# Moving VectorE's own sums, and the matmuls of other work, to other slots of a tanh-attention loop; attending in four key tiles at a time

## The chip, the cores and the metric

The kernel runs on one core of one Trainium2 chip. The metric is the device time of one execution in microseconds; three runs of the kernel before gave a median of 6138.88 us (6137.63 to 6139.3).

## What is computed

The input x is 8 images of 128 channels on a 36 x 36 grid. Layer 0 is a convolutional attention block with a residual. Layer 1 takes each image as 1296 tokens of 128 features and adds an attention whose score is a sum of tanh over the features, and then an expert-choice feed-forward layer. The part that takes most of the time is layer 1's attention:

```python
q = jnp.einsum('bld,ed->ble', x, Wq) + bq
k = jnp.einsum('bld,ed->ble', x, Wk) + bk
t = jnp.tanh(q[:, :, None, :] + k[:, None, :, :])
scores = jnp.einsum('bijd,d->bij', t, w) + bw[0]
attn = jax.nn.softmax(scores, axis=-1)
return jnp.einsum('bij,bjd->bid', attn, x)
```

For every image there are 1296 x 1296 pairs of tokens, and for each pair 128 values of tanh. Everything is float32.

## The kernel before

**The scores.** The kernel doesn't evaluate tanh pair by pair. It splits the features into small groups, of 5 and of 6 features, and writes the sum over a group as one fraction: a denominator and a numerator that are each a matrix product of a query factor (qf, two parts) with a key factor (kf). A group of 5 has 32 rows to contract over, a group of 6 has 64. The scores of a pair are the sum of all numerators divided by their denominators. The work is cut into *units*: one image b, one chunk c of 432 queries (three an image), one tile j of 128 keys (ten an image, and a remainder of 16 keys). A full unit has 12 *slots* k (`SLOTS`, L49 to L54); each slot does two groups at once on different rows of TensorE's array. They come in threes: k % 3 = 0 and 1 are groups of 5 (L53), k % 3 = 2 is groups of 6 (L54). A remainder unit has only two slots. The whole loop has 2928 slots (L1113).

**One slot.** The order of the instructions is written out by hand (L102). In slot p, `take_turns` (L1072) first lets other work copy out a result; then `numerators(p)` (L977) issues the matmuls n for this slot; `denominators(p + LAG)` (L960) issues the matmuls d three slots ahead, and on ScalarE the logarithm of d and, every second slot, the exponential of its negative, which is the reciprocal lq; `terms(p, ns)` (L982) multiplies n by lq on VectorE; and `matmul_turn` (L1077) lets other work issue matmuls.

**The sums.** `terms` has two ways. In the slots of `DVE_PAIRS` (L59), the groups of 6, VectorE multiplies the two numerators in place in PSUM and adds both into a running sum accd (L996 to L999). The first of these in a unit starts accd and has one addition less (L990 to L994). In the other eight slots VectorE multiplies out of PSUM into a buffer rp (three of them, L147), and GpSimd adds rp to a second running sum, accp (L1006 to L1012): the first rp is kept (k = 0), the second makes accp (k = 1). After a unit, `sums` (L1016) adds the halves of accp and accd on GpSimd, and ScalarE takes the exponential seven slots later (L1146, L1026). For a remainder unit, matmuls do the sum (`rem_scores`, L1039), issued in the following unit; they read rp.

**PSUM.** n and all the other work share four PSUM buffers (ps_n, L151): an n takes two, every other step takes one (`aux`, L159). The denominators have two buffers of their own (L149).

**The other work.** Behind the scores run generators in four lanes (L1067): query blocks and remainder sums (first_of_all), attending (urgent), gating (gates), and the next image's layer 0, tokens and keys (background). Each step issues a few matmuls into one aux buffer, yields `TAKE`, copies the result out one slot later at the earliest, and yields `matmuls()`. `take_turns` lets no lane but first_of_all copy in a slot of DVE_PAIRS. `matmul_turn` lets none but first_of_all issue matmuls in the slot before such a slot, nor while the balance is negative: every slot adds 400 (`PACE`), every matmul takes off its columns plus 20 (L282).

**Attending.** When all key tiles of a chunk have their exponentials, `attend` (L747) makes the weighted sum of the tokens, in four tiles of 108 queries. A tile needs 11 matmuls (10 key tiles and the remainder), issued by `weigh` (L737) in two parts, of 6 and of 5: the first part is copied to sums, the second added to it. For four tiles of the last chunk, early parts are done by `attend_early`.

Of the kernel before, what the change touches and what calls it, by code (L numbers as in the profile page):

```python
# [27 lines left out]
NKT = len(KT)  # L28
# [26 lines left out]
NP = len(SLOTS)  # L55
IN_TURN = [m + i for m in range(NF // 2) for i in (0, NF // 2)]
LAG = 3
SHIFT = 6.5
DVE_PAIRS = (2, 5, 8, 11)  # L59
PACE = 400  # L60


# [8 lines left out]
def kernel(  # L71
# [28 lines left out]
    nc = tc.nc  # L100
# [29 lines left out]
    with ExitStack() as loop, ExitStack() as score:  # L130
# [22 lines left out]
        def big_tile(name):  # L153
            return big.tile([128, NT * 128], F32, tag="big", name=name)
# [4 lines left out]
        def aux(name):  # L159
            return ps_n.tile([128, 512], F32, tag="n", name=name)  # L160
# [116 lines left out]
        def matmuls(rest=0):  # L277
            return (True, rest)
# [458 lines left out]
        def weigh(pa, i, some, es, xh, xr):  # L737

            for j in some:
                if j < NKT - 1:  # L740
                    e, v = es[j][:, i * T : (i + 1) * T], xh[:, j, :]
                else:
                    rows = slice(32 * i, 32 * i + REM)
                    e, v = es[j][rows, :T], xr[rows]
                bmm(pa, e, v, start=(j == some[0]), stop=(j == some[-1]))

        def attend(b, c, es):  # L747


            xh, _, xr = prepared[b]  # L750
            if c == 0:
                t2 = big_tile("t2").rearrange("p (t c) -> p t c", c=128)
                mv = two.tile([T, NT, 2], F32, tag="t2_mv", name="t2_mv")
                attended[b] = (t2, mv)
            t2, mv = attended[b]
            own = range(c * TPC, (c + 1) * TPC)
            for at in own:
                nc.sync.dma_start(t2[:T, at, :], tokd[b][at * T : (at + 1) * T])
            for i, at in enumerate(own):
                if i in early:  # L760
                    parts, sums = (order[NKT - 2 :],), early[i]
                else:
                    parts = (range(6), range(6, NKT))
                    sums = two.tile([T, C + 1], F32, tag="sums", name="sums")
                for some in parts:
                    pa = aux("pa1")[:T, : C + 1]
                    weigh(pa, i, some, es, xh, xr)
                    yield TAKE
                    if some[0] == 0:
                        nc.vector.tensor_copy(sums, pa)  # L770
                        yield matmuls()
                nc.vector.tensor_add(pa, pa, sums)
                inv = small.tile([T, 1], F32, tag="inv", name="inv")
                nc.vector.reciprocal(inv, pa[:, C : C + 1])
                nc.vector.scalar_tensor_tensor(
                    t2[:T, at, :], pa[:, :C], inv, t2[:T, at, :], ALU.mult, ALU.add
                )
                st = small.tile([T, 6], F32, tag="t2_st", name="t2_st")
                nc.vector.bn_stats(st, t2[:T, at, :])
                nc.vector.bn_aggr(mv[:, at, :], st)  # L780
                yield matmuls()
            if c == NCH - 1:
                prepared.pop(b)
            if b == NB - 1:
                yield from gate_logits(b, [c])

        def gating(b):
            yield from gate_logits(b, range(NCH))
            yield from gate_tokens(b)
# [114 lines left out]
        def residuals(n):  # L904

            for b in range(n):
                res.append(big_tile("res")[:, :N])
                nc.sync.dma_start(res[b], t2d[b])
                yield step()
# [11 lines left out]
        slots = []  # L921
# [4 lines left out]
        def prefetch(u):  # L926
            if u < len(units) and u not in kf_of:
                b, c, j = units[u]
                assert (b, j) in made
                n = 128 if j < NKT - 1 else 32  # L930
                kf = kfp.tile([128, NF, 128], F32, tag="kf", name="kf")
                nc.sync.dma_start(
                    kf[:, :, :n], kd[b][j].rearrange("p (q t) -> p q t", t=128)[:, :, :n]
                )
                kf_of[u] = kf
# [46 lines left out]
        def terms(p, ns):  # L982

            u, k = slots[p]
            lq = lq_of[u, k // 2]
            o = 2 * (k % 2)
            mult = nc.vector.tensor_mul
            rem = units[u][2] == NKT - 1
            if k in DVE_PAIRS and not rem:
                if k == DVE_PAIRS[0]:  # L990
                    live["d"] = acc.tile([128, CH], F32, tag="accd", name="accd")
                    mult(live["d"], ns[0], lq[:, o, :])
                    mult(ns[1], ns[1], lq[:, o + 1, :])
                    nc.vector.tensor_add(live["d"], ns[1], live["d"])  # L994
                else:
                    for h in range(2):  # L996
                        mult(ns[h], ns[h], lq[:, o + h, :])  # L997
                    for h in range(2):
                        nc.vector.tensor_add(live["d"], ns[h], live["d"])  # L999
            else:  # L1000
                rp = rpp.tile([128, 2, CH], F32, tag="rp", name="rp")
                for h, n in enumerate(ns):
                    mult(rp[:, h, :], n, lq[:, o + h, :])  # L1003
                if rem:
                    live.setdefault("rem", []).extend(rp[:, h, :] for h in range(len(ns)))
                elif k == 0:  # L1006
                    live["r"] = rp
                elif k == 1:
                    live["p"] = acc.tile([128, 2, CH], F32, tag="accp", name="accp")
                    nc.gpsimd.tensor_add(live["p"], live["r"], rp)  # L1010
                else:
                    nc.gpsimd.tensor_add(live["p"], live["p"], rp)  # L1012
            if k % 2 == 1:
                lq_of.pop((u, k // 2))
# [53 lines left out]
        balance = [0]  # L1068
# [3 lines left out]
        def take_turns(p, k):  # L1072
            for lane in lanes:
                if lane.due(p, False) and (k not in DVE_PAIRS or lane is first_of_all):
                    lane.run(p)

        def matmul_turn(p, k):  # L1077


            before = behind[0]  # L1080
            for lane in lanes:
                while lane.due(p, True) and behind[0] == before:
                    paced = balance[0] < 0 or k + 1 in DVE_PAIRS
                    if lane is not first_of_all and paced or lane is gates and urgent:
                        break
                    lane.run(p)
            balance[0] = min(balance[0] - (behind[0] - before) + PACE, 2 * PACE)
# [25 lines left out]
        for p, (u, k) in enumerate(slots):  # L1113
            b, c, j = units[u]
            rem = j == NKT - 1
            if k == 0:
                prefetch(u + 2)
                if c == 0 and j == 1:
                    if b > 0:
                        gates.append(gating(b - 1))  # L1120
                    if b == NB - 1:
                        gates.append(residuals(4))
                    if b + 1 < NB:
                        background.extend(
                            (normal(b + 1), conv_keys(b + 1), layer0(b + 1), tokens(b + 1),
                             keys(b + 1, range(NKT)))
                        )
            take_turns(p, k)
            ns = numerators(p)
            denominators(p + LAG)  # L1130
            terms(p, ns)
            if pending and pending[0][0] <= p:
                exps(p, *pending.popleft()[1:])
            last = p + 1 == len(slots) or slots[p + 1][0] != u

            if j == order[-1] and u + 1 < len(units) and k % 3:
                used = IN_TURN.index(SLOTS[k][0]) + 1
                if used < NF:
                    first_of_all.append(new_block(*units[u + 1][:2], IN_TURN[used]))
            elif j == order[-2] and last and u + 2 < len(units):  # L1140
                first_of_all.append(new_block(*units[u + 2][:2], IN_TURN[0]))
            matmul_turn(p, k)
            if last and rem:
                first_of_all.append(rem_scores(p, u, live.pop("rem")))
            elif last:
                pending.append((p + 7, u, sums(u)))  # L1146
        while pending:
            exps(p, *pending.popleft()[1:])
        take_turns(len(slots), 0)
        assert not first_of_all and not gates and not background  # L1150
        score.close()

# [205 lines left out]
```

The softmax here doesn't subtract the row's maximum and nothing guards it: scores larger than these inputs give would overflow.

## Time and profile before

| | |
|---|---|
| median of three runs | 6138.88 us |
| the profiled execution | 6140.74 us |
| its span, first to last instruction | 6139.0 us |
| before the first slot's numerators | about 162 us |
| the loop of 2928 slots | about 5824 us |
| the feed-forward layer after it | about 153 us |
| granted TensorE clock | 0.985 |
| numerators n, TensorE, 11520 matmul records | 3325.3 us busy |
| denominators d, TensorE, 11520 matmul records | 2991.6 us busy |
| products rp, VectorE, 3912 | 2173.3 us busy, 600 ns each |
| products n in place, VectorE, 1440 | 814.9 us busy, 608 ns each |
| additions to accd, VectorE, 1440 | 866.3 us busy, 602 ns each |
| additions to accp, GpSimd, 1440 | 2915.8 us busy, 2025 ns each |
| logarithms, ScalarE, 2928 | 2524.2 us busy, 878 ns each |
| exponentials of reciprocals, ScalarE, 1464 | 2398.2 us busy, 1638 ns each |

How to read the views: PE is TensorE's matmuls, PEld its weight loads, DVE is VectorE, ACT ScalarE, POOL GpSimd. A float32 matmul stands in the trace as two records, two passes over the same columns. In a line of time, the first number is the start in us from the span's start, the second the time from the first start to the last end of the instructions merged in it, and "x4" their number; at the end, in brackets, is how long the engine was idle and what ended that. In the list of waits, a line names the waiting engine, tile and line, then what it waited for, the time in all, how often, and the longest.

### The profile page before, as it was taken

What the parts mean: (1) busy time and instruction counts of PE and PEld (TensorE: products, weight loads), DVE (VectorE), ACT (ScalarE), POOL (GpSimd) and SP (SyncE); (2) the same over time, 40 slices, a digit from 0 to 9 for tenths busy, and PEclk for the clock granted to TensorE, in tenths of its full rate; (3) what the DMA queues carried; (4) which work ended last, traced back from release to release, by engine and by line L of the source; (5) the groups of instructions that cost most, each with busy time, mean ns of one, the idle gap of its engine ahead of it and who ended that gap; (6) DMA issues with size and microseconds to landing.
All of it is one profiled execution on the core that took longest, in us unless ns stands there. A gap on an engine that the chain in (4) does not pass through costs nothing.

```text
span 6139.0 us, 93072 instructions
## 1 busy us (share of the span) xinstructions
PE 5957.9 (97%) x33480; PEld 2862.1 (47%) x33480; DVE 4796.4 (78%) x9521; ACT 5279.9 (86%) x5371; POOL 4597.7 (75%) x2819
## 2 busy tenths in 40 slices
PE   7999999999999999999999999999999999999996
PEld 5454444544544445444455444454444544544443
DVE  4787878877788787877888777887778877788882
ACT  1888898888988888889998889888898888999990
POOL 4777777777787777778778786877777777787870
PEclk9999999999999999999999999999999999999997
DMA  1210011100110002100111001110011100110008
GB/s 44 70 37 22 25 62 38 34 25 28 68 43 20 26 27 71 39 24 23 44 55 39 22 24 59 44 39 22 20 65 40 34 25 28 58 50 29 28 20 297
DMA packets 151519, 270.87 MB, mean 44 GB/s; under 512 B 45648, under 2 KB 76752, under 8 KB 151056
## 3 DMA queue, kind: packets, MB, share of 16 engines
q1 hardware_dynamic: 151056, 264.92, 13.0%
q8 instruction: 264, 4.33, 0.3%
q14 instruction: 199, 1.63, 0.1%
HBM read 200.41 MB, written 64.19 MB: 43 GB/s over the span
## 4 chain that ended last, share of the span: by engine, by line
PE 77%; ACT 7%; DVE 6%; issue 6%; POOL 2%; DMA 1%; SPq 0%; DVEq 0%; POOLq 0%; ACTq 0%
PE n L949 37%; PE d L949 12%; PE pa L284 7%; PE pc L284 5%; ACT lq L972 5%; PE s L284 3%; PE pk L284 3%; PE pq L284 3%; DVE rp L1003 2%; DVE n L997 1%; DVE accd L999 1%; PE d L954 1%; ACT lq L975 1%; DMA w<-in_weight_dram 1%; PE n L954 1%
## 5 line engine op out<-in xcount | busy, mean ns | idle before, releaser
L1012 POOL TENSOR_TENSOR accp<-accp,rp 128x864 f32<-128x864 f32 x1440 | 2915.8, 2025 | 1041.0 <-DVE rp L1003 948.8
L949 PE MATMUL n<-qf,kf 32*128 32x432 f32 (+1 forms) x11520 | 3325.3, 574 | 46.5 <-ACT e L1032 13.3
L949 PE MATMUL d<-qf,kf 32*128 32x432 f32 (+1 forms) x11520 | 2991.6, 561 | 38.7 <-ACT lq L972 38.2
L972 ACT ACTIVATE lq<-d 128x864 f32<-128x864 f32 x2928 | 2524.2, 878 | 542.6 <-PE d L949 512.1
L1003 DVE TENSOR_TENSOR rp<-n,lq 128x432 f32<-128x432 f32 x3912 | 2173.3, 600 | 743.5 <-PE d L949 542.8
L975 ACT ACTIVATE lq<-lq 128x1728 f32<-128x1728 f32 (+1 forms) x1464 | 2398.2, 1638 | 46.3
L949 PEld LDWEIGHTS n<-qf,kf 32*128 32x128 f32 (+1 forms) x11520 | 1206.4, 184 | 1600.3 <-DVE rp L1003 581.5
L949 PEld LDWEIGHTS d<-qf,kf 32*128 32x128 f32 (+1 forms) x11520 | 1090.0, 185 | 422.1 <-issue 224.7
L997 DVE TENSOR_TENSOR n<-n,lq 128x432 f32<-128x432 f32 x1440 | 814.9, 608 | 142.1 <-PE n L949 88.5
L999 DVE TENSOR_TENSOR accd<-n,accd 128x432 f32<-128x432 f32 x1440 | 866.3, 602 | 24.6
L1010 POOL TENSOR_TENSOR accp<-rp 128x864 f32<-128x864 f32 x240 | 485.2, 2022 | 197.7 <-DVE rp L1003 195.6
L711 POOL TENSOR_SCALAR qf<-qf,cs_s 128x432 f32<-128x432 f32 x192 | 260.9, 1365 | 45.0 <-ACT qf L710 44.4
L284 PEld LDWEIGHTS pa<-xh,e 128*108 128x108 f32 x1920 | 222.5, 174 | 131.1 <-DVE rp L1003 56.0
L1021 POOL TENSOR_TENSOR accd<-accp,accd 128x432 f32<-128x432 f32 x240 | 265.2, 1105 | 18.8
L1019 POOL TENSOR_TENSOR accp<-accp 128x432 f32<-128x432 f32 x240 | 264.4, 1102 | 16.7
L284 PE MATMUL pa<-xh,e 128*108 128x129 f32 x1920 | 262.9, 283 | 8.7 <-ACT e L1032 5.2
L284 PE MATMUL s<-q,k 128*116 128x432 f32 x480 | 230.3, 568 | 1.7 <-DVE q L316 1.4
L284 PEld LDWEIGHTS pk<-xT,a_k 128*128 128x128 f32 x1408 | 171.2, 192 | 107.0 <-DVE n L997 33.7
L462 POOL TENSOR_TENSOR tot<-tot,e 116x432 f32<-116x432 f32 x192 | 212.0, 1104 | 6.0 <-ACT e L471 4.6
L471 ACT ACTIVATE e<-s 116x432 f32<-116x432 f32 x240 | 124.9, 520 | 98.3 <-PE s L284 97.9
L284 PE MATMUL pa<-e,vw 116*128 116x432 f32 x480 | 204.6, 549 | 0.0
L284 PE MATMUL pk<-xT,a_k 128*128 128x128 f32 (+1 forms) x1408 | 202.5, 287 | 0.1
(213 smaller groups left out, 3788.4 us busy)
## 6 DMA issues: line engine op xcount, KB each, us to landing
kf<-kd SPq DMA_DIRECT2D x239, 512.0 KB
kd<-ks SPq DMA_DIRECT2D x158, 256.0 KB
w<-in_weight_dram SPq DMA_DIRECT2D x32, 1024.0 KB
wk_t<-wk_t_d SPq DMA_DIRECT2D x7, 768.0 KB
wv_t<-wv_t_d SPq DMA_DIRECT2D x7, 768.0 KB
wq_t<-wq_t_d SPq DMA_DIRECT2D x7, 768.0 KB
x<-in_x_dram SPq DMA_DIRECT2D x8, 648.0 KB
t<-tokd SPq DMA_DIRECT2D x96, 54.0 KB
```

Of the source, the lines that this page charges most:

```text
L284: mm(out, lhsT, rhs, **kw)
L711: nc.gpsimd.tensor_scalar(qf[:, 1, :], qf[:, 0, :], cs_s[:, q : q + 1], None, ALU.mult)
L949: mm(outs[h][:, :CH], kf[rows[h], q, :], qf_of[b, c, q][rows[h], part, :], start=True, stop=True)
L972: nc.scalar.activation(lq[:, o : o + n, :], d[:, :n, :CH], AF.Ln)
L975: nc.scalar.activation(some, some, AF.Exp, scale=-1.0)
L997: mult(ns[h], ns[h], lq[:, o + h, :])
L999: nc.vector.tensor_add(live["d"], ns[h], live["d"])
L1003: mult(rp[:, h, :], n, lq[:, o + h, :])
L1010: nc.gpsimd.tensor_add(live["p"], live["r"], rp)
L1012: nc.gpsimd.tensor_add(live["p"], live["p"], rp)
L1019: nc.gpsimd.tensor_add(s[:, 0, :], s[:, 0, :], s[:, 1, :])
L1021: nc.gpsimd.tensor_add(d, s[:, 0, :], d)
```

## The change

The slots of VectorE's own sums become the first of each three, k = 0, 3, 6, 9, groups of 5. GpSimd's sums then begin at k = 1 and k = 2. Since other work may issue no matmuls in the slot ahead of these, its matmuls now come in k % 3 = 0 and 1 and no longer in the groups of 6; the comparison wraps at the unit's end. The two slots of a remainder unit count as places 1 and 11 for the lanes. Attending is done in three parts, of 4, 4 and 3 key tiles, with the middle one added to sums by one more instruction on VectorE; the four tiles with early parts keep theirs.

```diff
-DVE_PAIRS = (2, 5, 8, 11)
+DVE_PAIRS = (0, 3, 6, 9)
...
-                    parts = (range(6), range(6, NKT))
+                    parts = (range(4), range(4, 8), range(8, NKT))
...
-                    if some[0] == 0:
-                        nc.vector.tensor_copy(sums, pa)
+                    if some is not parts[-1]:
+                        if some is parts[0]:
+                            nc.vector.tensor_copy(sums, pa)
+                        else:
+                            nc.vector.tensor_add(sums, pa, sums)
                         yield matmuls()
...
-                elif k == 0:
+                elif k == 1:
                     live["r"] = rp
-                elif k == 1:
+                elif k == 2:
                     live["p"] = acc.tile([128, 2, CH], F32, tag="accp", name="accp")
...
-                    paced = balance[0] < 0 or k + 1 in DVE_PAIRS
+                    paced = balance[0] < 0 or (k + 1) % NP in DVE_PAIRS
...
-            take_turns(p, k)
+            place = (1, NP - 1)[k] if rem else k
+            take_turns(p, place)
...
-            matmul_turn(p, k)
+            matmul_turn(p, place)
...
-        take_turns(len(slots), 0)
+        take_turns(len(slots), 1)
```

## The prediction

> **Names.** A slot is one pair of numerator matmuls n(p), the denominators d(p+3) issued right after it on TensorE, and VectorE's products for p. Three slots make a *three*: 5a and 5b (groups of 5, 32-row matmuls) and 6 (group of 6, 64-row). A *behind step* is the background, attending or query-block work that TensorE does between two slots; its result is copied out in the next slot. The *pair slot* is the one of each three in which VectorE multiplies in place in PSUM and then adds both halves into accd (DVE_PAIRS); in the other two it multiplies into rp and GpSimd adds.
>
> **What bounds the kernel now.** First the page: its shares of busy time and its chain.
>
> ```profile
> PE 5957.9 (97%) x33480; PEld 2862.1 (47%) x33480; DVE 4796.4 (78%) x9521; ACT 5279.9 (86%) x5371; POOL 4597.7 (75%) x2819
> ...
> PE 77%; ACT 7%; DVE 6%; issue 6%; POOL 2%; DMA 1%; SPq 0%; DVEq 0%; POOLq 0%; ACTq 0%
> ```
>
> TensorE carries the chain, but its 97% includes matmuls that started and then stood. So next I read the waits, for what TensorE stands on before n.
>
> ```profile
> POOL accp L1012 <- DVE rp L1003: 948.8, 648, 6.9
> PEld n L949 <- DVE rp L1003: 581.5, 1032, 1.5
> ...
> PEld n L949 <- DVE accd L999: 198.5, 472, 1.6
> ...
> DVE rp L1003 <- PE rem L1045: 22.2, 24, 1.1
> ```
>
> Numerators wait for VectorE to free their PSUM buffers: there are four, an n takes two, a behind step takes one. GpSimd mostly waits for work. Last, one three in order of time, with a behind step (pc) in slot 6 and one in 5a. TensorE:
>
> ```profile
> 1066.35 0.99 PE L949 MATMUL n<-qf,kf 64*128 64x432 f32 x4
> ...
> 1068.01 1.27 PE L284 MATMUL pc<-xwin,wk_t 128*128 128x198 f32 x6
> 1069.21 0.65 PE L949 MATMUL n<-qf,kf 32*128 32x432 f32 x2
> ...
> 1070.26 1.27 PE L284 MATMUL pc<-xwin,wk_t 128*128 128x198 f32 x6
> 1071.46 0.63 PE L949 MATMUL n<-qf,kf 32*128 32x432 f32 x2
> ...
> 1072.40 1.00 PE L949 MATMUL n<-qf,kf 64*128 64x432 f32 x4
> ```
>
> and VectorE in the same stretch:
>
> ```profile
> 1067.55 1.12 DVE L997 TENSOR_TENSOR n<-n,lq 128x432 f32<-128x432 f32 x2
> 1068.58 1.24 DVE L999 TENSOR_TENSOR accd<-n,accd 128x432 f32<-128x432 f32 x2
> 1069.73 0.34 DVE L312 COPY k<-pc 128x187 f32<-128x187 f32 x1
> 1070.30 1.12 DVE L1003 TENSOR_TENSOR rp<-n,lq 128x432 f32<-128x432 f32 x2 [0.23 <-PE n L949]
> ```
>
> Differences of starts give TensorE's prices: slot 6 takes 1.66 us (1066.35 to 1068.01), a pc step 1.20, a 5 slot 0.94 (1071.46 to 1072.40). VectorE's: the pair slot starts at 1067.55; the first half is free when the first add ends, 1068.58 + 0.60 = 1069.18, 1.63 us after the pair's start; the whole pair takes 2.27. That is the point of this profile: n of 5a starts at 1069.21, when **two things end together**, the behind step and the first add. Slot 6 plus its behind step (2.86 us) covers the pair's hold on PSUM almost exactly. Over the whole trace, of 518 5a slots after such a pair, 260 have the second n starting 55 ns after the first add's end; so that wait is real and comes last half the time.
>
> I sorted 959 threes by which slots have behind steps and averaged the time between the n's. None: 138, 4.75 us. Only 6: 106, 5.49. Only 5a: 66, 4.82. Both: 508, 6.34. All three: 87, 6.84. Others: 54, about 6.3. Prologue (162 us) and tail (153 us) don't change.
>
> **What the Trainium skill says.** "Trainium Kernel Development and Optimization", Performance Expectations: matmul busy time is a poor measure, because matmuls are pipelined. The trace agrees: 97% busy, with 581.5 us of waits on rp inside. "TensorEngine Tiling (Array Packing)", Key Properties: a change of tiling mode drains TensorE. It agrees: inside a mode passes start 0.36 us apart, but a 5 slot's second passes start at 1071.93 and slot 6 only at 1072.40. "TensorE: Matmul & The Clock Gate", Part 3: matmuls start in program order, only weight loads move ahead. So a second n that waits holds up both d's and the behind step after it. The trace shows it: at 1069.21 the d's start after the n's.
>
> **The change, part by part.** (1) *The pair slot moves from 6 to 5a; behind steps move from (6, 5a) to (5a, 5b).* The amounts of work and the number of mode changes in a three stay the same; what covers the pair's hold changes. Start 5a at 0. Its n's end at 0.99, and the pair starts at 1.09 (as 1069.21 to 1070.30). First add ends: 1.09 + 1.63 = 2.72; the second n of 5b starts 0.055 later, 2.78. TensorE has been done with 5a (0.94) and its behind step (1.20) at 2.14: it stands **0.64 us**. The buffers leave no way round: two are held by the pair, one by the behind step (its copy is queued behind the pair on VectorE, as the 0.34 us COPY at 1069.73 is now), one by 5b's first n. Then 5b 0.94, its behind step 1.20, slot 6 1.66: 2.78 + 3.80 = 6.58 us, against 6.05 in the three shown. Slot 6's own n's don't wait: their buffers come free at about 4.6, before 4.92. One pair in four is the first of its unit (L990 to 994): it writes straight into accd and frees its first half after one multiplication, so there only TensorE's work counts, 2.14 + 3.80 = 5.94. Mean: (3 x 6.58 + 5.94)/4 = 6.42.
>
> The 6.34 measured for "both" holds longer steps and stray waits, 0.29 above 6.05. Some of these go: n of slot 6 waits on rp now, with no behind step ahead of it (its stretch to the next behind step averages 1.96 us against 1.65 at best); afterwards it has one. I keep 0.09 of the 0.29, bounds 0 and 0.29. So 6.51: +0.17 x 508 = **+86 us** (bounds +41 and +188).
>
> The other threes by the same steps. *None*: slot 6's second n now needs the pair's second half, at 1.09 + 2.27 + 0.06 = 3.42, and runs 1.64 from there: 5.06; first pairs about 4.6; mean 4.95, +0.20 x 138 = +28. *Only 6* becomes only 5a: 5b at 2.78, slot 6 at about 3.85 (the copy comes after the pair), 5.5: +0. *Only 5a* becomes only 5b: the step itself now waits for a buffer until 2.78, then 1.20 + 1.66 = 5.64, first ones 5.0; mean 5.45: +0.6 x 66 = +40. *All three*: 2.78 + 0.94 + 1.0 + 1.66 + 0.92 = 7.3, first ones 6.8; about 7.15: +0.3 x 87 = +26. Others, +0.25 x 54 = +14. Sum of part 1: **+194 us**.
>
> (2) *GpSimd's order.* The last rp of a unit now comes in slot 12, so one 2.02 us addition comes ahead of the two 1.10 us ones of sums. The exp of the unit is issued 7 slots (14 us) later, which hides it; without that cover 2 us x 240 would show. Value 0. The qf multiplications on GpSimd's queue stand one addition later; GpSimd waits 949 us for rp, so 0 (bounds 0 and +20).
>
> (3) *Behind the remainder unit* rp's buffer is taken over at k = 2 instead of k = 1, and by then the rem matmuls are done: the 22.2 us of "rp <- PE rem" go. VectorE is not always last there: -15 (bounds -22 and 0).
>
> (4) *Attending in 4, 4, 3.* The 11 matmuls of a tile are the same. 92 of the 96 tiles (4 keep their early sums) get one more step: one add, 0.29 us on VectorE by the row of its neighbour (pa <- pa,sums, 292 ns), 27 us in all, at 78% load partly beside TensorE; and one more pair of mode changes, about 0.2 us of TensorE, 18 us. No DMA is added. Shorter steps fit the pace of 400 a slot better (596 twice in three slots against 894). I take +20 (bounds -20 and +60).
>
> **Sum.** 194 - 15 + 20 = +199. The profiled execution lasted 6140.74 us (span 6139.0); that is 2 us from the median 6138.88, so I add to the median and round: **6340 us**. With the bounds of the parts, 6230 to 6430. A measurement tells about 0.2%, 12 us, from no change.
>
> **Rivals.** *A, an evener TensorE (faster).* Now slot 6 carries 1.66 plus a behind step and 5b nothing; afterwards 5a and 5b carry a step each and slot 6 none: 2.14, 2.14, 1.66 against 2.86, 2.14, 0.94. If PSUM's hold doesn't bind, "both" falls to TensorE's own 5.94 and slot 6's waits on rp go: -0.40 x 508 = -203; with (3) and (4), 5940; half of it 6040. For it: the 581.5 us of waits on rp. Against: the pair's 1.63 us to its first free buffer. It decides where the wait of 5b's second n stays under about 0.25 us, which needs behind steps in 5a of 1.6 us or more; most are 0.9 to 1.3. Chance 0.22.
>
> *B, the waits only move.* What n of slot 6 loses (0.31 us in some 600 slots, 186 us) pays for what n of 5b gains (0.64 x 3/4 x 508 = 244 us, less where steps are long): about 6140. Chance 0.06.
>
> *C, the behind work no longer fits.* 92 more steps with 2 of 3 slots open to them: some are left over at a chunk's end, where they run one after another with TensorE waiting for each copy. At 92 x 1.5 us more than forecast, about 6480. Chance 0.06.
>
> **Chances and range.** Forecast 0.66, A 0.22, B 0.06, C 0.06. Slower by over 0.2%: 0.66 + 0.06 = 0.72; within: 0.06; faster: 0.22. From 6090 (half of A's cases lie above or near it) to 6430 leaves out about 0.2.
>
> **What would show it.** "PEld n <- DVE accd L999" should grow from 198.5 us to over 350, at 5b, about 0.6 us each; "PEld n <- DVE rp" should fall from 581.5 to under 400; "rp <- PE rem" should vanish; the pair still takes 2.27 us. In a three with two steps, slot 6 should last 1.66 us, 5b start near 2.8 after 5a, and the three take near 6.5. I am wrong if 5b's second n follows the behind step at once, if threes with both take under 6.3 us, or if the waits on rp fall by more than those on accd grow.

## The result, and the profile after

The changed kernel takes 6374.07 us (median of four runs, 6368.71 to 6374.97), the kernel before 6139.09 us on the same chip: a ratio of 1.0382, 95% interval 1.0369 to 1.0395, so 235 us slower. The forecast was 6340, with a range from 6090 to 6430. The granted TensorE clock of the profiled executions, 0.985 before and 0.982 after, differs by 0.3%, far less than the 3.8%.

The page's shares of busy time and its chain, after the change:

```profile
PE 6087.0 (96%) x33480; PEld 2884.0 (45%) x33480; DVE 4824.6 (76%) x9613; ACT 5312.7 (83%) x5371; POOL 4597.7 (72%) x2819
...
PE 83%; DVE 10%; ACT 3%; issue 2%; DMA 1%; POOL 1%; SPq 0%; DVEq 0%; POOLq 0%; ACTq 0%
```

The work is nearly the same as before: TensorE has as many matmul records, VectorE 92 instructions and 28 us more, GpSimd exactly its 4597.7 us. The chain has moved from 77% TensorE and 6% VectorE to 83% and 10%. Next, the waits:

```profile
POOL accp L1015 <- DVE rp L1006: 1208.8, 834, 7.6
...
PEld n L952 <- DVE rp L1006: 450.9, 886, 1.5
...
PEld n L952 <- DVE accd L1002: 399.9, 671, 2.0
```

The numerators' wait for the additions into accd has doubled from 198.5 us, and that for rp has fallen by 131. To see where it happens, here is one three of the changed kernel in order of time, with a pc step in 5a and one in 5b. TensorE:

```profile
1110.56 0.63 PE L952 MATMUL n<-qf,kf 32*128 32x432 f32 x2
1110.57 0.63 PE L952 MATMUL d<-qf,kf 32*128 32x432 f32 x2
...
1111.49 1.27 PE L284 MATMUL pc<-xwin,wk_t 128*128 128x198 f32 x6
1112.70 1.20 PE L952 MATMUL n<-qf,kf 32*128 32x432 f32 x3
1113.28 0.63 PE L952 MATMUL d<-qf,kf 32*128 32x432 f32 x2
...
1114.21 1.27 PE L284 MATMUL pc<-xwin,wk_t 128*128 128x198 f32 x6
1115.41 0.99 PE L952 MATMUL n<-qf,kf 64*128 64x432 f32 x4
...
1117.06 0.63 PE L952 MATMUL n<-qf,kf 32*128 32x432 f32 x2
```

and VectorE:

```profile
1111.58 1.13 DVE L1000 TENSOR_TENSOR n<-n,lq 128x432 f32<-128x432 f32 x2 [0.47 <-PE d L952]
1112.62 1.24 DVE L1002 TENSOR_TENSOR accd<-n,accd 128x432 f32<-128x432 f32 x2
```

The first n of 5b starts at 1112.70, as soon as the step is over. The second, and with it both d's, starts at 1113.28: the first addition ends at 1112.62 + 0.60 = 1113.22. The merged n line is long (1.20) and the d's are 0.58 us late. The page counts TensorE as busy all the same: the two passes of the first n (1112.70 and 1113.16) run alone, where in the slot 5a above two n's and two d's start within 0.02 us of each other. So a share of busy time of 96% does not tell that TensorE does less in that time. The three takes 6.50 us, where the one shown of before took 6.05.

Adding up all slots from the starts of the matmuls gives the whole difference (us; "n and d" is the time from a slot's first n to its step or to the next slot):

| part of the loop | before | after | difference |
|---|---|---|---|
| n and d in 5a, 960 slots | 1068 | 988 | -80 |
| n and d in 5b, 960 slots | 1130 | 1538 | +409 |
| n and d in 6, 959 slots | 1881 | 1810 | -71 |
| remainder slots | 103 | 103 | 0 |
| behind steps | 1642 | 1615 | -27 |
| loop | 5823 | 6054 | +231 |

All of the loss lies in 5b, the slot right behind the pair; the other parts gain 178 us.

### The profile page after: what moved, and what is told of

It is laid out like the page before. It is cut to its first block, busy times and chain, and to the rows that moved or that the text cites. A ratio compares the mean times of both kernels' runs of the same rounds, so it can differ in the third digit from the quotient of the medians.

```text
span 6372.4 us, 93017 instructions
## 1 busy us (share of the span) xinstructions
PE 6087.0 (96%) x33480; PEld 2884.0 (45%) x33480; DVE 4824.6 (76%) x9613; ACT 5312.7 (83%) x5371; POOL 4597.7 (72%) x2819
## 4 chain that ended last, share of the span: by engine, by line
PE 83%; DVE 10%; ACT 3%; issue 2%; DMA 1%; POOL 1%; SPq 0%; DVEq 0%; POOLq 0%; ACTq 0%
PE n L952 43%; PE d L952 14%; PE pa L284 8%; PE pc L284 5%; DVE n L1000 4%; PE s L284 3%; PE pk L284 3%; PE pq L284 3%; DVE accd L1002 2%; ACT lq L975 1%; PE d L957 1%; PE n L957 1%; DMA w<-in_weight_dram 1%; DVE accd L997 1%; DVE accd L995 1%
## 5 line engine op out<-in xcount | busy, mean ns | idle before, releaser
L1015 POOL TENSOR_TENSOR accp<-accp,rp 128x864 f32<-128x864 f32 x1440 | 2913.9, 2024 | 1293.1 <-DVE rp L1006 1208.8
L952 PE MATMUL n<-qf,kf 32*128 32x432 f32 (+1 forms) x11520 | 3426.1, 574 | 93.0 <-DVE accd L1002 65.1
L952 PE MATMUL d<-qf,kf 32*128 32x432 f32 (+1 forms) x11520 | 2938.6, 563 | 35.9 <-ACT lq L975 35.4
L952 PEld LDWEIGHTS n<-qf,kf 32*128 32x128 f32 (+1 forms) x11520 | 1185.9, 185 | 1710.1 <-DVE rp L1006 450.9
L995 DVE TENSOR_TENSOR accd<-n,lq 128x432 f32<-128x432 f32 x240 | 145.7, 607 | 195.4 <-PE d L952 185.8
L284 PE MATMUL pa<-xh,e 128*108 128x129 f32 x1920 | 286.2, 287 | 7.5 <-ACT e L1035 7.4
```

Of the source, the lines that this page charges most:

```text
L284: mm(out, lhsT, rhs, **kw)
L952: mm(outs[h][:, :CH], kf[rows[h], q, :], qf_of[b, c, q][rows[h], part, :], start=True, stop=True)
```

## The experiments

**Part by part.** Attending alone, in the kernel before:

```diff
-                    parts = (range(6), range(6, NKT))
+                    parts = (range(4), range(4, 8), range(8, NKT))
```

> The kernel before with only the attending changed, to turns of 4, 4 and 3 key tiles. The theory (the loss comes from where the pair slot stands) has the attending as a side matter: within 40 us of 6139, on the record +20 for 92 more steps; the two traces hint at less, since TensorE's stretches with attending sum to 346 us before and 297 us after, which would make it about 6110. The rival, that the loss lies in the 92 added steps and their additions, wants most of the 235 us here: 6300 or more.

Measured: 6186.22 us, ratio 1.0084 (1.0069 to 1.0099). It costs 50 us, more than the +20 of the prediction and more than the 40 allowed here, and against the -27 that the sums suggested. In its trace n and d in 5a take 55 us more and the steps 27; why the turns cost that much stays open. The slots alone, which is the changed kernel with this line put back:

> The changed kernel with attending put back to parts of 6 and 5: only the slots are moved. The theory: all of the loss is here, 6350 to 6410. The rival (attending is the loss): near 6150.

Measured: 6345.25 us, ratio 1.0341 (1.0326 to 1.0356). So 209 of the 235 us belong to the slots, and attending adds some 26 beside them, half of what it costs alone.

**The hold on PSUM, by the order in the pair.** The changed kernel with

```diff
                     for h in range(2):
                         mult(ns[h], ns[h], lq[:, o + h, :])
-                    for h in range(2):
                         nc.vector.tensor_add(live["d"], ns[h], live["d"])
```

> The changed kernel with the pair slot's four VectorE instructions in another order: multiply, add, multiply, add in place of multiply, multiply, add, add. The first PSUM buffer comes free some 1.27 us after the pair's start, not 1.64, the second at about the same 2.3. The theory, that 5b's second numerator waits for the first addition: it then starts about 0.37 us earlier in some 455 threes, -170 us, so about 6210. If TensorE stands for another reason (the denominators, ScalarE, the place of the other work as such), 6374 stays, or rises by up to 25 us for the dependent pairs of instructions.

Measured: 6373.19 us, ratio 1.039 (1.0375 to 1.0406): no gain, where the theory wanted 6210. The time alone speaks for the rival, that TensorE stands for another reason. The trace tells where the gain went. TensorE in the same place as above:

```profile
1112.82 0.82 PE L952 MATMUL n<-qf,kf 32*128 32x432 f32 x2
1113.02 0.63 PE L952 MATMUL d<-qf,kf 32*128 32x432 f32 x2
...
1114.18 1.27 PE L284 MATMUL pc<-xwin,wk_t 128*128 128x198 f32 x6 [0.16 <-DVE accd L1001]
```

The second n does start earlier, as expected: in threes with both steps its median went from 2.72 to 2.34 us after 5a's start, and n and d in 5b fell by 127 us in all. But 5b's own step needs the pair's *second* buffer, and now stands for that (the 0.16 in brackets); the pair lasts 2.42 us instead of 2.28 (medians), and n and d in slot 6 grew by 105 us, the steps by 39. So the wait for the first buffer got shorter as the theory has it, and as much came back behind it: in 5b's step it is the wait for the second buffer; what makes slot 6 longer was not followed up.

**The hold taken away by writing to SBUF.**

```diff
-                        mult(ns[h], ns[h], lq[:, o + h, :])
+                        mult(lq[:, o + h, :], ns[h], lq[:, o + h, :])
...
-                        nc.vector.tensor_add(live["d"], ns[h], live["d"])
+                        nc.vector.tensor_add(live["d"], lq[:, o + h, :], live["d"])
```

> The changed kernel with the products of the pair slot written over lq in SBUF and not in place in PSUM; the additions read them there. Each PSUM buffer is free after its multiplication, 0.6 and 1.1 us after the pair's start, as in the other slots. The theory: the 361 us that 5b's second numerators stand behind their first go, and threes with two steps fall to TensorE's own 5.9 to 6.1 us: 6000 to 6070, under the kernel before. A rival, that the slots of groups of 5 are simply too short with two steps beside them (TensorE's own work): 6300 or more. Another, that lq held longer delays ScalarE: the gain is eaten, 6200 to 6350.

Measured: 7083.9 us, ratio 1.1538 (1.1505 to 1.1572). It went the other way, for a reason that neither theory had. First the additions after the change, then those of this run:

```profile
L1002 DVE TENSOR_TENSOR accd<-n,accd 128x432 f32<-128x432 f32 x1440 | 867.5, 602 | 24.7
```

```profile
L1002 DVE TENSOR_TENSOR accd<-lq,accd 128x432 f32<-128x432 f32 x1440 | 1520.1, 1056 | 24.7
```

The second number behind the bar is the mean of one in ns: with both inputs in SBUF an addition takes 1056 instead of 602, and VectorE's busy time rose by 771 us (more on this in the last section). So this run doesn't decide about the hold.

**The hold taken away by leaving work out**, in both layouts:

```diff
                     for h in range(2):
                         mult(ns[h], ns[h], lq[:, o + h, :])
-                    for h in range(2):
-                        nc.vector.tensor_add(live["d"], ns[h], live["d"])
```

(and the same for the first pair's addition). The groups of the pair slots are then missing from the scores; the runs are for their times alone.

> The kernel before without the additions into accd in the pair slots (they are left out, so those groups are missing from the scores): VectorE only multiplies there. The PSUM buffers come free 0.6 and 1.1 us after the pair's start, and VectorE has 1.15 us less work in a three. The theory: in the layout of before the second numerators stood 101 us behind the first after later pairs; these go, and some waits on rp with them: about 5950, between 5850 and 6050.

> The changed kernel with the same additions left out, to be set beside the one above. The theory, that the changed kernel loses by PSUM buffers that the pair holds too long for a slot of 5: with the hold down to 0.6 us the wait goes and threes with two steps take TensorE's own 5.9 us, so about 5950, within 60 us of the kernel above; the 235 us between the two layouts are gone, the 50 us of attending in more steps perhaps not. If the layout loses for another reason (mode changes, query blocks, ScalarE), this one stays 150 us or more above the other.

Measured: 6046.75 us in the layout of before (ratio 0.9859, 0.9844 to 0.9873) and 5937.38 us in the changed one (0.9678, 0.9664 to 0.9692). Both lose the same VectorE work; the first gains about 90 us, the second 437, and **the order of the two turns round**: the changed layout is 109 us ahead, where the expectation had them within 60. In it the second n's after a pair with a step stood 397 us behind the first with the additions and 51 us without; threes with both steps fell from 6.47 to 5.97 us, near TensorE's own 5.94. In the layout of before the same figures are 105 and 23 us, 6.34 and 6.22. A pc step in 5a and the slot 5b in the changed layout without the additions, where n and d start together again:

```profile
1042.36 1.27 PE L284 MATMUL pc<-xwin,wk_t 128*128 128x198 f32 x6
1043.56 0.63 PE L952 MATMUL n<-qf,kf 32*128 32x432 f32 x2
1043.57 0.63 PE L952 MATMUL d<-qf,kf 32*128 32x432 f32 x2
```

This pair of runs separates the theories best: without the additions the changed layout is the better one, and with them it loses. Leaving them out takes away the long hold on PSUM and 1.2 us of VectorE's time per pair at once. The run on the layout of before takes away the same time and gains much less, but the two layouts need not feel VectorE's time equally; the next experiment but one shortens the hold and adds to VectorE's time.

**Another slot of 5.** The changed kernel with attending put back to 6 and 5, the pair slot at 5b, steps in 5b and 6:

```diff
-DVE_PAIRS = (0, 3, 6, 9)
+DVE_PAIRS = (1, 4, 7, 10)
...
-                elif k == 1:
+                elif k == 0:
                     live["r"] = rp
...
-            place = (1, NP - 1)[k] if rem else k
+            place = (2, NP - 1)[k] if rem else k
...
-        take_turns(len(slots), 1)
+        take_turns(len(slots), 0)
```

> As the kernel with only the slots moved, attending in 6 and 5, but the pair slot is the second group of 5 (k = 1, 4, 7, 10), and behind steps go into slots 5b and 6. The theory says that any slot of 5 with one step behind it (0.94 + 1.2 us) is too short for the pair's hold (2.7 us): 0.6 us of wait, now before the second numerator of slot 6, and 6.5 us a three; about the 6345 of the pair slot at 5a, 6290 to 6420. If it was 5a in particular, or that slot 6 has no step behind it, near 6140.

Measured: 6264.59 us, ratio 1.0212 (1.0197 to 1.0227). The mechanism is there: of 575 second numerators of slot 6 after later pairs with a step, 530 start about 55 ns after the first addition's end, and threes with both steps take 6.52 us. The time is still 81 us under that of the pair at 5a and below the range I gave, because threes with one step or none are shorter (4.97 and 5.47, and 4.81, where the pair at 5a has 5.53, 6.25 and 5.15). My theory here spoke of threes with both steps only; it was too coarse for the others.

**One half in SBUF.** On the kernel with only the slots moved, and on the kernel before:

```diff
-                    for h in range(2):
-                        mult(ns[h], ns[h], lq[:, o + h, :])
-                    for h in range(2):
-                        nc.vector.tensor_add(live["d"], ns[h], live["d"])
+                    mult(lq[:, o, :], ns[0], lq[:, o, :])
+                    mult(ns[1], ns[1], lq[:, o + 1, :])
+                    nc.vector.tensor_add(live["d"], ns[1], live["d"])
+                    nc.vector.tensor_add(live["d"], lq[:, o, :], live["d"])
```

> The kernel with only the slots moved (attending in 6 and 5), where in the later pairs the first half's product is written over lq in SBUF, the second's in place, then the second is added and the first last. The first PSUM buffer is free after 0.6 us, the second after about 1.65, and one addition a pair has both inputs in SBUF; such additions took 1056 ns in the mean where both were so, against 602 with one input in PSUM. The theory: 5b's second numerator no longer waits (-250 us or so from 6345), and 720 additions give back up to 0.45 us each where VectorE comes last: about 6200, between 6100 and 6350. If PSUM's hold is not what binds, only the slower additions show: over 6345.

> The kernel before with the same mixed pair: first product over lq in SBUF, second in place, the first's addition last. Here the wait to be won is small (101 us in all behind first numerators), and the slower additions meet the same VectorE: 6150 to 6350, so the mixed pair should help the layout with the pair at 5a and not this one.

Measured: 6528.4 us (ratio 1.064, 1.0625 to 1.0654) and 6466.81 us (1.0543, 1.0527 to 1.0559). By their times alone the first would speak for the rival. Its trace doesn't: the first buffer is free early though VectorE has more to do, and 5b's second numerators stand 35 us behind the first in all (later pairs with a step), against 359 without this edit; n and d in 5b fell from 1488 to 1110 us. So it is the hold, and not VectorE's time, that 5b stands for. But slot 6 grew from 1814 to 2174 us and the steps by 138, while VectorE has slower additions: one kind beside the other, in the same kernel,

```profile
L1002 DVE TENSOR_TENSOR accd<-lq,accd 128x432 f32<-128x432 f32 x720 | 755.3, 1049 | 25.0
...
L1001 DVE TENSOR_TENSOR accd<-n,accd 128x432 f32<-128x432 f32 x720 | 437.3, 607 | 24.9
```

and in the layout of before:

```profile
L999 DVE TENSOR_TENSOR accd<-lq,accd 128x432 f32<-128x432 f32 x720 | 1041.4, 1446 | 25.0
```

That a pair with one half in SBUF would help one layout and not the other was wrong: it harms both, and both times lie outside the ranges given.

**The other order in the kernel before.**

> The kernel before with the pair's order multiply, add, multiply, add. The first buffer is free 0.37 us earlier, the whole pair lasts 0.15 us longer. The theory: in this layout the second numerator of 5a ends its wait together with the behind step, so an earlier first buffer helps in the half of the threes where it was last, and the longer pair costs where the second buffer or VectorE was last: 6090 to 6150. A hold that binds nowhere in this layout: 6139 to 6180.

Measured: 6143.07 us, ratio 1.0008 (1.0002 to 1.0015), 0.1%: nothing to be won there. Both ranges of the expectation include this time, so it doesn't decide between them. In the trace 5a's second n's stand 36 us behind the first instead of 102, n and d in 5a fell by 54 us, and those in 5b grew by 56: here too the wait only moves on.

**The two moves apart.** VectorE's sums at 5a, the steps left in 6 and 5a:

```diff
+HELD = (2, 5, 8, 11)
...
-                if lane.due(p, False) and (k not in DVE_PAIRS or lane is first_of_all):
+                if lane.due(p, False) and (k not in HELD or lane is first_of_all):
...
-                    paced = balance[0] < 0 or (k + 1) % NP in DVE_PAIRS
+                    paced = balance[0] < 0 or k + 1 in HELD
...
-            place = (1, NP - 1)[k] if rem else k
+            place = k
...
-        take_turns(len(slots), 1)
+        take_turns(len(slots), 0)
```

> The changed kernel with the behind steps left where they were, in slots 6 and 5a; only VectorE's sums (and GpSimd's) go to 5a. Copies now also come in 5a, ahead of the pair. The theory: 5b's second numerator waits for the first addition as in the changed kernel, at 2.8 us or a little later; slot 6 then waits for the copy behind the pair: 6.6 to 6.8 us in threes with two steps, about 6420, no better than 6350. If it was moving the behind steps off the groups of 6 that cost the time, most of it comes back: under 6230.

Measured: 6485.72 us, ratio 1.0575 (1.0558 to 1.0593), 66 us over the 6420 expected and worse than the whole change; 509 of 535 second numerators of 5b behind a step start about 55 ns after the first addition. And the sums left at 6, the steps moved to 5a and 5b:

```diff
-DVE_PAIRS = (0, 3, 6, 9)
+DVE_PAIRS = (2, 5, 8, 11)
+HELD = (0, 3, 6, 9)
...
-                if lane.due(p, False) and (k not in DVE_PAIRS or lane is first_of_all):
+                if lane.due(p, False) and (k not in HELD or lane is first_of_all):
...
-                    paced = balance[0] < 0 or (k + 1) % NP in DVE_PAIRS
+                    paced = balance[0] < 0 or (k + 1) % NP in HELD
...
-                elif k == 1:
+                elif k == 0:
                     live["r"] = rp
-                elif k == 2:
+                elif k == 1:
```

> The other half of the change: the pair slot stays at 6, the behind steps go to 5a and 5b (attending in 4, 4, 3). Copies come in 5b and 6. The theory: slot 6 now has no step behind it to cover the pair's hold: its own 1.66 us are over, and the second numerator of 5a waits for the first addition at about 2.85 us, a wait of 1.2; then 0.94, 1.2, 0.94 and 1.2 us: 7.1 us a three with two steps, about 6700 in all, between 6550 and 6800, worse than the whole change. If steps off the groups of 6 were good in themselves and only the pair's move bad: 6250 or less.

Measured: 6201.62 us, ratio 1.0103 (1.0086 to 1.012), against an expectation of 6700, and in the range (6250 or less) that it gave to the other reading: steps off the groups of 6 do no harm by themselves, and the pair's move alone is bad. So it is by the times: attending in 4, 4, 3 alone has 6186, within 0.3%. TensorE and then VectorE in one of its threes, from the start of slot 6:

```profile
1117.29 0.99 PE L953 MATMUL n<-qf,kf 64*128 64x432 f32 x4
...
1118.94 0.63 PE L953 MATMUL n<-qf,kf 32*128 32x432 f32 x2
...
1120.01 1.27 PE L285 MATMUL pc<-xwin,wv_t 128*128 128x198 f32 x6
```

```profile
1118.32 1.13 DVE L1001 TENSOR_TENSOR n<-n,lq 128x432 f32<-128x432 f32 x2 [0.56 <-PE n L953]
1119.36 1.24 DVE L1003 TENSOR_TENSOR accd<-n,accd 128x432 f32<-128x432 f32 x2
```

5a's numerators start at 1118.94, 1.65 us after slot 6's, while the pair is still multiplying. They don't wait. My expectation had miscounted the buffers: with no step in the pair slot, the pair holds two of the four and the next slot's numerators take the *other two*. The first to need a pair's buffer is then 5a's step, at 1120.01, just after the first addition ends (1119.36 + 0.60 = 1119.96). By then slot 6's rest and all of 5a have covered the hold, at a cost of some 0.1 us.

So the loss comes with the pair's move to a slot of 5, and what decides is when one of its buffers is first wanted. The pair holds its first buffer for 1.63 us, until 2.7 to 2.8 us after its slot's start. With a step in the pair slot, the step takes the third buffer and the next slot's second n wants the pair's first: after 2.14 us behind a slot of 5, after 2.86 behind one of 6. With no step there, the next slot's step is the first to want it: after two slots of 5, 1.88 us; after one of 6 and one of 5, 2.60. Behind a slot of 6 both come about when the first addition ends; behind a slot of 5 neither does. The changed kernel shows the second case too: in the 100 threes whose only step is in 5b, n and d in 5b take 1.93 us before the step starts, twice a slot's own 0.94, and 1.41 in the 99 such threes without the additions.

## Why the prediction was right

**The place and the size of the wait.** The text had 5b's second n at 2.78 us after 5a's start; the median after the change is 2.72 behind later pairs with a step. Of 532 such numerators, 506 start 40 to 70 ns after the first addition's end; before, 266 of 521 did. The second n's stand 388 us in all behind the first, against 102. (The 455 and 361 us in the expectations come from a count that misses some 50 of these numerators.)

**The threes.** With both steps: forecast 6.51, measured 6.47. First pairs of a unit: 5.94 and 5.95; later ones 6.58, and 6.44, 6.69 and 6.84 at k = 3, 6 and 9. None: 4.95 and 5.08; only 5a: 5.5 and 5.71; only 5b: 5.45 and 5.63; all three: 7.15 and 7.10.

**Luck.** That 6.51 came so close is in part luck. The forecast gave every step the 1.20 us of a pc step, and the two steps of a three take 2.07 us in the mean, 0.33 less. The three slots take 0.39 more than its 0.94, 1.42 and 1.66 (the mean over first and later pairs): 1.03, 1.54 and 1.84, so slot 6's n's do wait, against the text. The two nearly cancel, and the 0.09 kept for stray waits covers the rest. The threes with one step or none are 0.13 to 0.21 us longer than worked out, 53 us in all, and those with both 21 us shorter. All threes together are 220 us longer than before, where the forecast's parts add up to 199; 11 us more lie in steps behind the remainder slots and 4 outside the loop, which makes the 235. The stated bounds of the parts, added up, would give 6246 to 6515; 6230 to 6430 does not follow from them, and the time lies inside either.

**Counts.** One reading of the trace was off. In the kernel before the last record of an attending step runs beside the next slot's n, and I counted some 70 such slots as having a step of their own. There were some 1481 steps before and 1574 after, 93 more, as 92 tiles with one more step want. The effect on the sum was small: with the counts of after, the forecast's times give 5909 us for all threes, 199 more than the 5710 before, and 194 was forecast.

**The change of tiling mode.** The lines cited for it separate less than the text says: in the same slot of 5 the first and second passes, of one mode, start at 1071.46 and 1071.93, as far apart as the second and slot 6 at 1072.40. Over the trace of before, passes in the midst of a mode start 0.33 to 0.36 us apart in the median, and both the last pass ahead of a change and the first behind it 0.47. Only the 18 us of (4) rest on this.

**Attending** came out over the forecast: +20 (bounds -20 and +60), +50 alone and some +26 beside the moved slots.

**GpSimd's order**: 0 forecast; its busy time is the same to 0.1 us, and the exponentials wait 8.3 us for it in all, where 6.2 were. **The remainder**: nothing waits for the rem matmuls any more, as forecast, where 22.2 us were. The 24 threes right behind a remainder unit took 172 us before and 131 after, 41 less, where -15 was forecast (bounds -22 and 0); how much of that is the rem matmuls was not measured by itself.

**The signs.** The wait on accd was to pass 350 us (399.9); that on rp was to fall under 400 and fell to 450.9, a sign that was missed. It fell by 131, less than the 201 by which that on accd grew. A waiting n does keep the two d's behind it, as the text took from the order of the matmuls: in the three shown they start at 1113.28 with the second n.

**The rivals.** A, the evener TensorE, describes this layout rightly where the hold is gone: 5937 us without the additions, against the 5940 I gave it; but there VectorE also has less to do, so that the two numbers agree proves little. B had the right sign for slot 6 and 5a (-151 us) but not its size beside +409. C is not to be seen: the steps' sum fell by 27 us.

## What to carry to other kernels

When buffers go round between engines, count for each user which earlier user's buffer it gets, and compare the time until then with how long that user holds it; a long hold costs little where the work until then covers it, and shows where it doesn't. Evening out the busy engine's slots paid here only with the hold of the other engine gone: the changed layout was 235 us slower than the old one with the additions, and 109 us faster when both went without them. And count again for every variant, since leaving one user out of a slot changes who waits for whom. A shorter hold is not yet a shorter time either: twice the wait moved on to the next user.

## What the runs showed of the hardware

VectorE's float32 addition of 128 x 432 takes 602 to 608 ns in the mean with one input in PSUM, and 1049, 1056 and 1446 ns with both inputs in SBUF (one half in SBUF with the slots moved, both halves, one half in the layout of before). It is waiting and not work, and GpSimd is what it waits for: in the first of these runs, 148 of the 720 such additions have no GpSimd instruction beside them and take 607 to 610 ns; 389 have one beside them for all of their first 600 ns and take 1367 in the mean, up to 2826. Of the 451 that take over 700 ns, 438 end 0.46 to 0.48 us after a GpSimd instruction has ended. In the same kernel the additions with one input in PSUM take 606 to 609 ns whatever GpSimd does. GpSimd's own additions into accp stay at 2024 to 2037 ns in these runs, 2024 in the changed kernel.

The Trainium skill, "SBUF — State Buffer", Who interferes with whom, says that a VectorE instruction with two SBUF inputs contends with a GpSimd instruction that reads SBUF, over a port pair that only one of them has at a time. These runs agree. Multiplying in place in PSUM thus has two sides here: it holds the buffers, and it keeps the additions out of GpSimd's way.
